# The first tiles of an S4 + int4-FFN block: dequantized weights scaled in 64-column operations, products split by pass, and a new written-out order on five engines

## The chip, the cores and the metric

The kernel runs on one core of one Trainium2 chip, as one launch. The metric is the time of one execution in device microseconds; the figure for the kernel before is the median of three such times. A profiled execution gives, besides, a trace of every instruction and DMA with start and duration.

Engine names are those of the profile: PE is the matrix engine (PEld its weight loads), DVE the vector engine, ACT the scalar engine, POOL the GpSimd engine, SP the engine that issues the DMAs. Instructions of one engine run in the order in which they stand.

## The reference: what is computed

`x` has 2048 rows of 1024 columns. With `xn = layernorm(x)` the result is

```python
x = x + s4(xn) + ffn(xn)
# ffn: the weights are int4, in groups of 64 with a scale and a zero each
w = (w - zero[:, :, None]) * scale[:, :, None]
g = jnp.einsum('bsh,ih->bsi', x, Wg)
u = jnp.einsum('bsh,ih->bsi', x, Wu)
h = jax.nn.silu(g) * u
return jnp.einsum('bsi,hi->bsh', h, Wd)
```

`s4` is a causal convolution of each row with a kernel of length 1024 made from S4 parameters, plus `D * xn`. The inner size of the FFN is 2752, that is 21 tiles of 128 rows of the weights (`j` = 0 to 20) and one half tile ("mix").

## The kernel before

**Precision.** Each fp32 operand is kept as a pair of fp16 numbers, high and low part. A product is three matmuls ("passes", `PASS = ((0, 0), (0, 1), (1, 0))`): weight high times x high, weight high times x low, weight low times x high. A pair is made by a cast on ACT (high) and a subtraction on DVE (low = value minus high).

**Stages.** (1) Rows of x are loaded, normalized and turned so that the hidden dimension lies on the partitions. (2) Gate and up products for all `j`: `j` = 0 and 1 as plain matmuls, from `j` = 2 on by a Strassen-like scheme with seven products over 2x2 blocks. (3) The convolution. (4) The down product. From stage 2's middle to the end, an order of the engines is written out or made by a planner; the change does not touch it.

**The first tiles.** The change is in the first 46 us. Here the first four x tiles (128 rows each, `n0` to `n3`, 512 KB) and the first four weight granules (`raw0` to `raw3`, 256 KB each; granules 0 and 1 are `j` = 0, granules 2 and 3 are `j` = 1, one per half of the contraction, `kq`) are made on the engines as follows.

- x tile `t`: `norm_stat(t)` on DVE (two bn_stats, one aggregate, and for `t` < 4 two small operations), a power on POOL, `scaled_x` on ACT, eight 128x128 transposes on PE into two PSUM banks, `early_hi(t)` (two casts on ACT), `early_lo(t)` (two subtractions on DVE).
- granule `gi`: `unpack` on DVE (two integer operations of 512 columns), scaling, eight transposes on PE, `early_w_hi` on ACT, `early_w_lo` on DVE.
- Scaling has three forms before: `scale_v` on DVE (two operations over all 1024 columns, with the scales broadcast, granules 0 and 3), `scale_part` on DVE (two operations over the first 12 groups, granule 1), and `scale_a` on ACT (one operation for each group of 64 columns, with scale and bias as one number per partition). `scale_a` and `scale_part` need `scale_c`, three small operations on POOL.
- `product(s, kq)`: the 24 matmuls of 128 columns of x tile `s` with granule `kq` of `j` = 0, for gate and up, with all three passes of each weight tile together. `j` = 1 follows as one block, `gate_up_plain(1, 0, 0, ...)`, 48 matmuls of 512 columns.

x tiles 4 to 15 go another way: `norm_stat` (DVE), power (POOL), `norm_hi` (ACT), `norm_lo` (DVE), and two DMA transposes for each tile on SP's queue.

**What sets the order.** Between `V.pin = A.pin = SP.pin = PE.pin = True` and `... = False` every operation of those engines is issued behind the one before it in the source: the order is the one written in the program (lines 941 to 1039 of before). POOL is not pinned. Behind this block a scheduler places the instructions at build time up to about 195 us; from there on a written order follows. Buffers limit it as well: `raw` and `w` have two buffers each, so the load of the third granule waits for the unpacking of the first, and the unpacking of the third for the transposes of the first; x tiles have eight buffers.

**Behind the block** come the rest of `j` = 0, 1 for x tiles 4 to 7 (`by_tile`), the mix granule, x tiles 8 to 15, `load_w` of granules 4 to 7 with DMA transposes (`wf<-nat` in the trace), and then `j` = 2 (`whole(2, 0)`), whose matmuls need granules 4 and 5, and `j` = 3, which needs 6 and 7.

Most operations are recorded through the class `Engine`, so that they all have line 82 (pinned) or 77 (not pinned) in the profile: the tile names tell them apart. `xt` and `wt` are the PSUM banks of the transposes, `wf` the turned weights, `x` the turned x, `n` the loaded x, `g` and `u` the gate and up banks, `nat` the weight pairs ahead of the DMA transposes.

Of the kernel before, what the change touches and what calls it, by code (L numbers as in the profile page):

```python
# [26 lines left out]
I32 = mybir.dt.int32  # L27
# [60 lines left out]
def build(nc, tc, x, xp, raw_d, sz_d, par_d, vct_d, tab_d, csrow_d, out):  # L88
# [3 lines left out]
    with es:  # L92
# [20 lines left out]
        def bank(name, tag="ps"):  # L113
            return psp.tile([P, 512], F32, tag=tag, name=name, **({} if tag == "ps" else {"bufs": 2}))

        V, A = Engine(tc, nc.vector), Engine(tc, nc.scalar)
        SP, G, PE = Engine(tc, nc.sync), nc.gpsimd, Engine(tc, nc.tensor)
# [32 lines left out]
        def xtile(cp, f):  # L150
            if (cp, f) not in xf:
                home, tag = (uxp, "ux") if f in (0, 1, 3) else (utp, "ut")
                xf[cp, f] = home.tile([P, 2, 4, 512], F16, tag=tag, name=f"x{cp}_{f}")
            return xf[cp, f]
# [17 lines left out]
        def fetch(*ts):  # L172
            for t in ts:
                xin[t] = utp.tile([P, 2048], F32, tag="ut", name=f"n{t}")
                for i in range(2 if t == 0 else 1):
                    part = slice(512 * i, 512 * i + 512) if t == 0 else slice(0, 1024)
                    SP.dma_start(xin[t][:, part], xp[t * P : (t + 1) * P, part])
# [38 lines left out]
        def turned(src, name):  # L216

            ps = bank(name).rearrange("p (a b) -> p a b", b=P)
            for b in range(4):
                PE.transpose(ps[:, b], src[:, P * b : P * b + P], ident)  # L220
            return ps

        def pair_hi(src, hi, name):
            ps = turned(src, name)
            A.copy(hi, ps)
            return ps
# [10 lines left out]
        def early_hi(t):  # L237
            xv, _ = halves(t)
            for i in range(2):
                f, sl = (3, 1, 7, 0)[2 * (t // 4 % 2) + i], slice(t % 4 * P, t % 4 * P + P)  # L240
                d = xtile(t // 8, f)
                early_x[t, i] = d[:, :, :, sl], pair_hi(xv[:, i], d[:, 0, :, sl], f"xt{t}_{i}")

        def early_lo(t):
            for i in range(2):
                d, ps = early_x.pop((t, i))
                los[t] = V.tensor_tensor(d[:, 1], ps, d[:, 0], ALU.subtract)
# [52 lines left out]
        with ea:  # L300
# [3 lines left out]
            def load_raw(gi):  # L304
                raw = wtemp("raw", [P, 16, 32], I32, f"raw{gi}")
                ld = SP
                ld.dma_start(raw, raw_d[gi].rearrange("p (a b) -> p a b", a=16))
                sz = wtemp("sz", [P, 2, 16], F32, f"sz{gi}")
                ld.dma_start(sz, sz_d[gi])
                return raw, sz  # L310
# [14 lines left out]
            def scale_v(w, sz):  # L325

                w3 = w.rearrange("p a b -> p (a b)")[:, 0:1024].rearrange("p (a b) -> p a b", a=16)
                bc = lambda k: sz[:, k].unsqueeze(2).to_broadcast([P, 16, 64])
                V.tensor_tensor(w3, w3.bitcast(I32), bc(1), ALU.subtract)
                V.scalar_tensor_tensor(w3, w3, WS, bc(0), ALU.mult, ALU.mult)  # L330

            def scale_c(gi, sz):

                G.tensor_scalar(sz[:, 0], sz[:, 0], WS, None, ALU.mult)  # L334
                G.tensor_tensor(sz[:, 1], sz[:, 1], sz[:, 0], ALU.mult)
                G.tensor_scalar(sz[:, 1], sz[:, 1], -1.0, None, ALU.mult)
                return sz

            def scale_part(w, sc, n):

                w3 = w.rearrange("p a b -> p (a b)")[:, 0 : 64 * n].rearrange("p (a b) -> p a b", a=n)
                bc = lambda k: sc[:, k, 0:n].unsqueeze(2).to_broadcast([P, n, 64])
                V.tensor_tensor(w3, w3.bitcast(I32), bc(0), ALU.mult)
                V.tensor_tensor(w3, w3, bc(1), ALU.add)
# [23 lines left out]
            def early_w_hi(gi, w):  # L368

                for i in range(2):  # L370
                    a = slice(4 * i, 4 * i + 4) if gi != G_MIX else slice(16 + 4 * i, 20 + 4 * i)
                    hi = wtile(0 if gi == G_MIX else gi)[:, a]
                    src = w.rearrange("p a b -> p (a b)")[:, 512 * i : 512 * i + 512]
                    early_w[gi, i] = pair_hi(src, hi, f"wt{gi}_{i}"), hi

            def early_w_lo(gi):
                for i in range(2):
                    ps, hi = early_w.pop((gi, i))
                    a = slice(8 + 4 * i, 12 + 4 * i) if gi != G_MIX else slice(16 + 4 * i, 20 + 4 * i)
                    V.tensor_tensor(wtile(1 if gi == G_MIX else gi)[:, a], ps, hi, ALU.subtract)  # L380
# [3 lines left out]
            def wtile(gi):  # L384
                if gi not in wft:
                    wft[gi] = wfp.tile([P, 28, P], F16, tag="wf", name=f"wf{gi}")
                return wft[gi]
# [196 lines left out]
            def plain(ps, w, cp, c, ts=slice(0, 512), kq=None, ends=None):  # L584


                xt = [xtile(cp, f) for f in ((3, 1), (7, 0))[c]]
                ks = [k for k in range(8) if kq in (None, k % 4 // 2)]
                first, last = ends or (0 in ks, 7 in ks)
                for k in ks:  # L590
                    for n, (wi, xi) in enumerate(PASS):
                        PE.matmul(ps[:, ts], w(k, wi), xt[k // 4][:, xi, k % 4, ts],
                                  start=(first and k == ks[0] and n == 0), stop=(last and k == ks[-1] and n == 2),
                                  **({"skip_group_check": True} if ends else {}))
# [104 lines left out]
            def plain_banks(j, cp, c):  # L699
                nm = f"{j}_{cp}{c}"  # L700
                return bank("g" + nm, "B"), bank("u" + nm, "D")

            def plain_part(banks, cp, c, wf, ts=slice(0, 512), kq=None, ends=None):
                for m, ps in enumerate(banks):
                    plain(ps, lambda k, wi: wf[k % 4 // 2][:, 8 * wi + 4 * m + k // 4 * 2 + k % 2, :], cp, c, ts, kq, ends)
# [238 lines left out]
            V.pin = A.pin = SP.pin = PE.pin = True  # L944
            busy, ones = bank("busy"), ident.bitcast(F16)
            for _ in range(24):
                PE.matmul(busy[:, 0:256], ones[:, 0:128], ones, start=True, stop=True)
            wt = {j: [wtile(2 * j), wtile(2 * j + 1)] for j in range(2)}
            first = plain_banks(0, 0, 0)

            def product(s, kq):
                plain_part(first, 0, 0, wt[0], slice(s * P, s * P + P), kq, ((s, kq) == (0, 0), (s, kq) == (3, 1)))

            fetch(0)
            rawt[0] = load_raw(0)
            rawt[1] = load_raw(1)
            fetch(1, 2)
            rawt[2] = load_raw(2)
            fetch(3)
            rawt[3] = load_raw(3)  # L960
            fetch(4, 5, 6, 7)
            rawt[G_MIX] = load_raw(G_MIX)
            xtile(0, 7)
            norm_stat(0)
            w0, s0 = unpack(0)
            scaled_x(0, 2)
            scale_v(w0, s0)
            w1, s1 = unpack(1)
            c1 = scale_c(1, s1)
            early_hi(0)  # L970
            early_w_hi(0, w0)
            norm_stat(1)
            scale_a(w1, c1, range(12, 16))
            early_lo(0)
            early_w_lo(0)
            product(0, 0)
            scaled_x(1)
            scale_part(w1, c1, 12)
            early_hi(1)
            fetch(8)  # L980
            early_w_hi(1, w1)
            early_lo(1)
            norm_stat(2)
            w2, s2 = unpack(2)
            c2 = scale_c(2, s2)
            product(1, 0)
            early_w_lo(1)
            product(0, 1)
            product(1, 1)
            scale_a(w2, c2, range(5))  # L990
            scaled_x(2)
            scale_a(w2, c2, range(5, 7))
            early_hi(2)
            fetch(9)
            w3, s3 = unpack(3)
            norm_stat(3)
            early_lo(2)
            product(2, 0)
            scale_a(w2, c2, range(7, 8))
            scaled_x(3)  # L1000
            scale_v(w3, s3)
            scale_a(w2, c2, range(8, 10))
            early_hi(3)
            fetch(10)
            product(2, 1)
            early_lo(3)
            scale_a(w2, c2, range(10, 16))
            early_w_hi(3, w3)
            product(3, 0)
            product(3, 1)  # L1010
            norm_stat(4)
            early_w_hi(2, w2)
            norm_stat(5)
            early_w_lo(3)
            early_w_lo(2)
            norm_hi(4)
            norm_hi(5)
            norm_lo(4)
            norm_stat(6)
            norm_hi(6)  # L1020
            norm_lo(5)
            fetch(11)
            norm_stat(7)
            norm_hi(7)
            norm_lo(6)
# [5 lines left out]
            early_w_hi(G_MIX, wq)  # L1031
# [5 lines left out]
            V.pin = A.pin = SP.pin = PE.pin = False  # L1037
# [19 lines left out]
            h0a = plain_h(first, 0, 0, 0)  # L1057
            h1a = gate_up_plain(1, 0, 0, wt[1])
# [557 lines left out]
```

## Time and profile before

| | us |
|---|---|
| median of three executions | 1281.69 (1280.97 to 1282.39) |
| the profiled execution, its own time | 1286.51 |
| its span in the trace | 1284.7 |
| PE busy | 1259.7 (98%) |
| DVE busy | 1020.2 (79%) |
| ACT busy | 676.5 (53%) |
| POOL busy | 184.3 (14%) |
| end of the first 46 us block on PE (last `u` matmul of `j` = 1, x tiles 0 to 3; start of the next block) | 45.89 |

PE is busy for nearly the whole span, so the time is PE's work plus PE's waits: 25 us of the span are not busy. A busy PE is not a PE at its peak: the clock it was granted is a column of its own. An engine's idle time is of interest only where PE, or a chain that PE later waits for, hangs on it.

### The profile page before, as it was taken

What the parts mean: (1) busy time and instruction counts of PE and PEld (TensorE: products, weight loads), DVE (VectorE), ACT (ScalarE), POOL (GpSimd) and SP (SyncE); (2) the same over time, 40 slices, a digit from 0 to 9 for tenths busy, and PEclk for the clock granted to TensorE, in tenths of its full rate; (3) what the DMA queues carried; (4) which work ended last, traced back from release to release, by engine and by line L of the source; (5) the groups of instructions that cost most, each with busy time, mean ns of one, the idle gap of its engine ahead of it and who ended that gap; (6) DMA issues with size and microseconds to landing.
All of it is one profiled execution on the core that took longest, in us unless ns stands there. A gap on an engine that the chain in (4) does not pass through costs nothing. (4 is left out here: it accounts for less than half of the span.)

```text
span 1284.7 us, 21385 instructions
## 1 busy us (share of the span) xinstructions
PE 1259.7 (98%) x8098; PEld 760.0 (59%) x8098; DVE 1020.2 (79%) x1391; ACT 676.5 (53%) x1219; POOL 184.3 (14%) x280
## 2 busy tenths in 40 slices
PE   7999899999999999999998999999999999999998
PEld 6644344444444444444443444467678888888887
DVE  7789975788888788779787886657669889779792
ACT  6777665665757656676576575620205433343330
POOL 2330010000010000101010001100000130366440
PEclk8999999999999999999998999999999999999999
DMA  6792829788895969799998998866868777999981
GB/s 233 195 209 50 184 92 207 191 227 207 207 252 133 266 148 247 192 224 248 238 243 198 260 246 185 251 231 200 307 201 317 254 236 217 257 288 257 289 175 50
DMA packets 358842, 276.59 MB, mean 215 GB/s; under 512 B 211851, under 2 KB 304851, under 8 KB 354643
## 3 DMA queue, kind: packets, MB, share of 16 engines
q1 hardware_dynamic: 336147, 263.17, 74.4%
q0 software_dynamic: 22016, 11.02, 7.1%
q8 instruction: 63, 1.03, 0.3%
q10 hardware_dynamic: 576, 1.05, 0.2%
q14 instruction: 40, 0.33, 0.1%
HBM read 132.88 MB, written 94.84 MB: 177 GB/s over the span
## 5 line engine op out<-in xcount | busy, mean ns | idle before, releaser
L82 PEld LDWEIGHTS <-wf 128*128 128x128 f16 x3000 | 287.3, 99 | 348.9 <-issue 11.5
L77 PEld LDWEIGHTS <-g 128*128 128x128 f16 x2940 | 287.6, 98 | 34.0 <-DVE g L77 0.6
L82 ACT ACTIVATE w<-w,sz 128x64 f32<-128x64 int32 x564 | 197.8, 428 | 66.8 <-DVE w L82 50.1
L82 PE MATMUL D<-x,wf 128*128 128x512 f16 x816 | 191.3, 385 | 2.2 <-ACT D L82 2.2
L77 PE MATMUL A<-b,g 128*128 128x256 f16 x1680 | 186.0, 273 | 0.3 <-DVE g L77 0.3
L82 PE MATMUL A<-x,wf 128*128 128x512 f16 x792 | 177.9, 380 | 5.0 <-DMA wf<-nat 4.6
L82 PE MATMUL C<-x,wf 128*128 128x512 f16 x804 | 179.1, 379 | 0.0
L77 ACT CAST g<-a 128x2560 f16<-128x2560 f32 x42 | 97.4, 2325 | 135.8 <-PE A L77 50.4
L82 DVE TENSOR_TENSOR w<-w 128x256 f32<-128x256 f32 (+1 forms) x244 | 132.7, 545 | 39.4 <-ACT w L82 32.3
L77 PEld LDWEIGHTS <-wf 128*128 128x128 f16 x960 | 86.0, 98 | 95.6 <-DMA wf<-nat 5.7
L77 DVE TENSOR_TENSOR g<-a,g 128x2560 f16<-128x2560 f32 x42 | 118.2, 2820 | 27.5 <-ACT g L77 27.5
L1468 POOL DMA_DIRECT2D out<-o x64 | 77.9, 2019 | 308.1 <-DVE o L77 288.3
L334 POOL TENSOR_SCALAR sz<-sz 128x16 f32<-128x16 f32 x43 | 19.4, 450 | 627.8 <-DMA sz<-in_sz 551.7
L82 ACT CAST nd<-w 128x896 f16<-128x896 f32 x70 | 65.3, 933 | 83.5 <-DVE w L82 70.0
L77 PE MATMUL D<-b,g 128*128 128x256 f16 x840 | 94.1, 273 | 0.0
L82 PE MATMUL B<-x,wf 128*128 128x512 f16 x396 | 90.9, 379 | 0.1
L82 DVE TENSOR_TENSOR nd<-w,nd 128x896 f16<-128x896 f32 x70 | 76.0, 1086 | 9.1 <-ACT nd L82 9.1
L82 ACT CAST nat<-w 128x896 f16<-128x896 f32 x62 | 55.3, 936 | 33.4 <-ACT B L82 17.0
L77 PEld LDWEIGHTS <-x 128*128 128x128 f16 x672 | 54.3, 98 | 20.9 <-issue 2.4
L82 DVE TENSOR_TENSOR nat<-w,nat 128x896 f16<-128x896 f32 x62 | 64.8, 1084 | 1.1 <-ACT nat L82 1.1
L77 DVE SCALAR_TENSOR_TENSOR p<-cv,p 128x512 f32<-128x512 f32 x32 | 22.0, 689 | 34.9 <-PE cv L77 23.4
L77 PE MATMUL cv<-band,x 128*128 128x256 f16 (+3 forms) x384 | 47.0, 272 | 2.0 <-DVE p L77 2.0
(181 smaller groups left out, 1451.1 us busy)
## 6 DMA issues: line engine op xcount, KB each, us to landing
a<-HF SPq DMA_DIRECT2D x28, 1280.0 KB, 7.4
WD<-nd SPq DMA_DIRECT2D x70, 448.0 KB, 4.0
b<-WD SPq DMA_DIRECT2D x49, 640.0 KB, 6.1
w<-SZT SPq DMA_DIRECT2D x80, 256.0 KB, 5.3
raw<-in_raw SPq DMA_DIRECT2D x65, 256.0 KB, 4.0
HF<-ha SPq DMA_DIRECT2D x54, 256.0 KB, 3.2
HF<-s SPq DMA_DIRECT2D x40, 256.0 KB, 3.2
HF<-hb SPq DMA_DIRECT2D x36, 256.0 KB, 3.2
```

What stands on the lines that cost most here:

```text
L77: return method(*args, **kw)
L82: self.last = method(*args, **kw)
L334: G.tensor_scalar(sz[:, 0], sz[:, 0], WS, None, ALU.mult)
L1468: G.dma_start(dst, o[:, q], accum_op=ALU.add)
```

## The change

It changes how the first four granules are scaled, in which order the first tiles are worked on, and how their products are cut; the mathematics stays.

- **Scaling.** `scale_v` and `scale_part` are gone. `scale_g` on DVE does one operation for each group of 64 columns: `w * a + b`, with `a` and `b` as one number per partition each. The groups are shared out anew: granule 0 has 16 groups on DVE; granule 1 has 8 on DVE and 8 on ACT; granule 3 has 10 and 6; granule 2 has 15 and 1. `scale_c` (POOL) is now needed for granules 0 and 3 too.
- **Loads.** The scales of granule 0 (`sz0`) go between the two halves of x tile 0, `raw0` behind both; x tile 1 is loaded ahead of `raw1`; granule 3 and x tile 3 are loaded ahead of granule 2.
- **Products** take a list of passes, so that the passes with a low part can stand behind others. `j` = 1 (`wide`) is cut into four pieces by granule and pass, inside the pinned block.
- **Order.** The order of all of these is new. x tile 3 and granule 3 come ahead of x tile 2 and granule 2. POOL is pinned as a fifth engine. The transposes of x tile 0 use banks of the tags B and D. 20 more filler matmuls (`busy`): 32 at the start, 12 ahead of the first product. `h0a` moves into the block.

By instruction: DVE loses 6 scaling operations (two of 1024 columns twice, two of 768) and gains 49 of 64 columns; ACT loses 5 of 64 columns; POOL gains 6 small ones; PE gains 20 filler matmuls with their weight loads; SP has the same 757 rows in another order. Behind about 195 us the order is the same on every engine.

```diff
-        SP, G, PE = Engine(tc, nc.sync), nc.gpsimd, Engine(tc, nc.tensor)
+        SP, G, PE = Engine(tc, nc.sync), Engine(tc, nc.gpsimd), Engine(tc, nc.tensor)
...
-            def scale_v(w, sz):
-
-                w3 = w.rearrange("p a b -> p (a b)")[:, 0:1024].rearrange("p (a b) -> p a b", a=16)
-                bc = lambda k: sz[:, k].unsqueeze(2).to_broadcast([P, 16, 64])
-                V.tensor_tensor(w3, w3.bitcast(I32), bc(1), ALU.subtract)
-                V.scalar_tensor_tensor(w3, w3, WS, bc(0), ALU.mult, ALU.mult)
...
+            def scale_g(w, sc, groups):
+
+                wv = w.rearrange("p a b -> p (a b)")
+                for g in groups:
+                    V.tensor_scalar(
+                        wv[:, 64 * g : 64 * g + 64], wv[:, 64 * g : 64 * g + 64].bitcast(I32),
+                        sc[:, 0, g : g + 1], sc[:, 1, g : g + 1], ALU.mult, ALU.add,
+                    )
...
-            for _ in range(24):
-                PE.matmul(busy[:, 0:256], ones[:, 0:128], ones, start=True, stop=True)
+            turning(32)
...
+            half_x = lambda i: SP.dma_start(xin[0][:, 512 * i : 512 * i + 512], xp[0:P, 512 * i : 512 * i + 512])
             fetch(0)
-            rawt[0] = load_raw(0)
+            half_x(0)
+            rawt[0] = load_raw(0, lambda: half_x(1))
+            fetch(1)
             rawt[1] = load_raw(1)
-            fetch(1, 2)
+            fetch(2)
+            rawt[3] = load_raw(3)
+            fetch(3)
             rawt[2] = load_raw(2)
-            fetch(3)
-            rawt[3] = load_raw(3)
             fetch(4, 5, 6, 7)
             rawt[G_MIX] = load_raw(G_MIX)
...
+            c0 = scale_c(0, sz[0])
             norm_stat(0)
-            w0, s0 = unpack(0)
             scaled_x(0, 2)
-            scale_v(w0, s0)
-            w1, s1 = unpack(1)
-            c1 = scale_c(1, s1)
+            w0 = unpack(0)[0]
+            scale_g(w0, c0, range(8, 16))
+            c1 = scale_c(1, sz[1])
+            scale_g(w0, c0, range(0, 8))
+            turn_w(0, w0)
+            norm_stat(1)
+            w1 = unpack(1)[0]
+            early_w_hi(0)
+            turn_x(0)
+            turning(12)
+            first = plain_banks(0, 0, 0)
+            early_w_lo(0)
             early_hi(0)
...
+            scale_a(w1, c1, range(8, 16))
+            scale_g(w1, c1, range(0, 8))
             early_lo(0)
+            w3 = unpack(3)[0]
+            product(0, 0, 2)
+            turn_w(1, w1)
+            c3 = scale_c(3, sz[3])
+            product(0, 0, 0, 1)
+            norm_stat(3)
             scaled_x(1)
...
+            product(1, 0, 1)
+            turn_x(3)
+            fetch(9)
+            scale_g(w3, c3, range(0, 8))
+            scale_a(w3, c3, range(10, 16))
+            early_hi(3)
             scaled_x(2)
+            product(1, 1, 0, 1)
+            early_lo(3)
+            norm_stat(4)
+            turn_w(3, w3)
+            early_w_hi(3)
+            norm_stat(5)
+            product(3, 1)
+            w2 = unpack(2)[0]
+            turn_x(2)
+            fetch(10)
+            product(3, 0)
             early_hi(2)
             early_lo(2)
+            norm_stat(6)
+            second = plain_banks(1, 0, 0)
+            wide(1, 0, 1)
+            scale_g(w2, c2, range(8, 16))
+            scale_g(w2, c2, range(0, 7))
+            norm_hi(4)
+            scale_a(w2, c2, range(7, 8))
             product(2, 0)
+            norm_hi(5)
+            early_w_lo(3)
             product(2, 1)
+            turn_w(2, w2)
             norm_lo(4)
             norm_hi(6)
             norm_lo(5)
+            early_w_hi(2)
+            norm_lo(6)
+            wide(1, 2)
+            early_w_lo(2)
+            wide(0, 0, 1)
+            h0a = plain_h(first, 0, 0, 0)
+            wide(0, 2)
             fetch(11)
             norm_stat(7)
             norm_hi(7)
...
-            h0a = plain_h(first, 0, 0, 0)
-            h1a = gate_up_plain(1, 0, 0, wt[1])
+            h1a = plain_h(second, 1, 0, 0)
```

In the program as built, DVE's order of the block after `product(1, 0, 0)` follows the same list; ACT has `h1a`'s Silu (which reads the last piece of `wide`) ahead of `norm_hi(7)`; SP has the store of `h1a` ahead of the two DMA transposes of x tile 7.

## The prediction

> **What bounds the kernel now.** I read the busy time by stages first. The stages are the first two, the written-out first block (to 46 us), what follows it, the four waits behind 131 us, and the long stretch to 477.
>
> ```profile
> 0.00:10.00 10.00, 6.97 (x40) 4.85 (x40) 5.77 (x12) 4.94 (x9) 4.52 (x13) 1.00 0.79 250
> 10.00:20.00 10.00, 7.01 (x56) 6.62 (x57) 8.10 (x15) 5.77 (x12) 1.26 (x4) 0.66 0.78 283
> 20.00:36.00 16.00, 13.61 (x191) 12.28 (x189) 14.69 (x31) 13.14 (x30) 4.01 (x11) 1.00 0.40 137
> 36.00:46.00 10.00, 10.00 (x50) 4.58 (x49) 6.52 (x11) 7.85 (x8) 2.81 (x6) 1.00 0.62 128
> 46.00:131.00 85.00, 85.00 (x542) 44.76 (x540) 75.61 (x109) 63.38 (x117) 15.71 (x36) 1.00 0.74 162
> 131.00:155.00 24.00, 20.76 (x94) 8.62 (x93) 23.56 (x30) 12.61 (x23) 0.00 (x0) 1.00 0.90 206
> 155.00:477.00 322.00, 321.59 (x1533) 147.53 (x1531) 257.17 (x417) 203.45 (x443) 21.75 (x58) 1.00 0.77 190
> ```
>
> The columns are PE, PEld, DVE, ACT, POOL, then PE's granted clock. PE lacks 8.4 us in the first 36 and none to 131; there it lacks 3.2 while DVE is full (23.56 of 24). From 155 to 477 PE is full again, so what is won or lost by 155 stays. The timeline of PE shows who is late at 131:
>
> ```profile
> 131.75 0.82 PE L77 MATMUL A<-x,wf 128*128 128x512 f16 x3 [0.24 <-DMA wf<-nat]
> 133.84 0.82 PE L77 MATMUL A<-x,wf 128*128 128x512 f16 x3 [1.26 <-DMA wf<-nat]
> 151.35 0.82 PE L77 MATMUL A<-x,wf 128*128 128x512 f16 x3 [0.86 <-DMA wf<-nat]
> 153.57 0.82 PE L77 MATMUL A<-x,wf 128*128 128x512 f16 x3 [0.75 <-DMA wf<-nat]
> ```
>
> PE waits here for the turned weights of granules 4 to 7. PE's own gain is therefore lost at this place unless the chain that makes them moves too. By the timelines of DVE and ACT that chain goes back without a break: DVE has hardly a gap from 83.94 (`norm_lo(15)`) to 148; before it `norm_stat`, POOL, `norm_hi` and `norm_lo` wait for one another in a loop; the loop begins with `norm_hi(8)` (54.25), behind the mix granule's 16 scalings on ACT (from 47.43), behind `norm_hi(7)` (45.21). So the question is when ACT starts `norm_hi(7)`.
>
> **The change part by part.** DVE's timeline prices the block:
>
> ```profile
> 5.34 0.21 DVE L82 TENSOR_SCALAR rs<-mv 128x1 f32<-128x1 f32 x2
> 5.47 0.75 DVE L82 TENSOR_SCALAR w<-raw 128x512 int32<-128x512 int32 x2
> ...
> 9.85 1.29 DVE L82 BATCH_NORM_STATS2 st<-n 128x6 f32<-128x512 f32 x2 [0.41 <-DMA n<-in_xp]
> ...
> 11.55 1.28 DVE L82 TENSOR_TENSOR x<-xt,x 128x512 f16<-128x512 f32 x2
> 12.74 1.28 DVE L82 TENSOR_TENSOR wf<-wt,wf 128x512 f16<-128x512 f32 x2
> ...
> 268.35 0.35 DVE L82 TENSOR_SCALAR s4n<-s4n,s4p 128x256 f32<-128x256 f32 x1
> 268.62 0.76 DVE L82 TENSOR_SCALAR w<-raw 128x512 int32<-128x512 int32 x2
> ```
>
> The first number is the start, the second the time from start to last end; operations overlap, so I price by starts. `norm_stat` takes 1.70 (9.85 to 11.55; 1.44 for tiles from 4 on, 30.86 to 32.30), a low pair 1.19, an `unpack` 0.67 (22.53 to 23.20).
>
> *The 64-column operation, T.* No row has it. Two operations of one column take 0.13, so 0.065 each; one of 512 columns 0.335; a column costs 0.53 ns. The only wide operation with a per-partition number (268.35) holds the next one off for 0.27; less 192 columns that is 0.17, so its number costs 0.07. The new form has two numbers. Bounds: 0.10 if they load beside the operation ahead; 0.24 if the second costs as much as the first; 0.32 if nothing overlaps (0.35 - 0.10 + 0.07). I take 0.17, the row it is nearest to.
>
> On the other side stands the Trainium skill, VectorE: DVE Perf Modes, section The TRN2 errata: a fixed cost per instruction, hence few large operations. Its 58 cycles plus half a cycle per column make 0.094 us for 64 columns, its measured 150 cycles 0.19; T by these would give a gain of 5.2 or 1.9 us below.
>
> *DVE.* Six operations go: two `scale_v` of 2.40 and `scale_part` of 2.01, together 6.8. 49 T = 8.3 come. DVE gets 1.5 us more work, and what changes the end is the order. In the built order DVE is never held from its first `unpack` on: each cast that it needs ends 0.7 us or more ahead (ACT has its pairs of casts at 0.5 each half; the closest are the casts of granule 1, ending 17.1, needed 17.8). From there to the first low half of x tile 2, which PE needs: four unpacks 2.7, three full `norm_stat` 5.1, two short 2.9, five low pairs 5.95, half a pair 0.6, and 34 of the 49 scalings (16 + 8 + 2 + 8): 17.25 + 34 T = 23.05.
>
> *The start.* `sz0` comes ahead of x tile 0's second half, whose issue moves by one (0.47 on SP). Landing is by bandwidth (0.98 between the halves before), so the delay lies between 0 and 0.47; I take 0.13, the size of a 16 KB load beside 256 KB in 0.98, doubled. The first `unpack` starts at 5.6. POOL's `scale_c(0)` stands ahead of the power of tile 0: 0.9 (12.10 to 13.00) when DVE is not on SBUF, 3.1 when it is (6.42 to 9.49). From `sz0`'s landing at about 4.5 (issue 1.20 plus the median 3.3) it ends between 5.4 and 7.6, with DVE's first scaling at 6.3 behind it; at 4.5 DVE does bn_stats, beside which the short price holds (24.28). I take nothing, and at worst 1.3.
>
> *x tile 1 sooner.* It removes the 0.41 at 9.85; one 256 KB load less in front is worth 0.8 at the 310 GB/s of that stretch, so it lands near 9.0, and `norm_stat(1)` is due at 5.6 + 0.7 + 16 T = 9.0. Nothing is left over.
>
> *PE.* From 28.65 it runs through: `wide(1, 0, 1)` 16 x 0.216 = 3.46, two products 48 x 0.056 = 2.69, eight transposes 0.92, `wide(1, 2)` 1.73, `wide(0, 0, 1)` 3.46, `wide(0, 2)` 1.73: 13.99, end 42.65 (durations: 22 matmuls 36.39 to 41.14, 12 in 0.67 at 32.17). Covers: granule 2's last scaling on DVE is at 33.3, due 34.8; its low pair at 39, due 40.9. Before, the same point is 45.89: 3.2 us sooner. The 32 and 12 fillers lie in time in which PE waits for DVE: without that cover 20 more would cost 3.9 (0.195 each, 24 in 4.68).
>
> *Clock.* In 10 to 20 us PE was granted 0.66, after gaps of 1.92 and 0.93; 22 matmuls and 16 transposes cost about 2.4 us more there. In the new order DVE sets PE's pace to 28.65, so I count nothing. The Trainium skill (TensorE: Matmul & The Clock Gate, Part 1) has half clock after an idle window of 3.4 us, which the fillers would avoid; by it, too, no term changes.
>
> *New waits.* ACT: `h1a`'s Silu, which needs `wide(0, 2)`, stands ahead of `norm_hi(7)`; ACT idles from 37 to 42.65 with it, and `norm_hi(7)` starts at 43.3 (0.6 for the Silu) instead of 45.21: 1.9 gained of PE's 3.2. SP: the store of `h1a` (44) stands ahead of x tile 7's transposes, which need `norm_lo(7)` (46.7) anyway. `raw2` waits for the second unpack (11.5) with x tiles 4 to 7 behind; four loads at 1.87 issue and 6.3 landing are there by 20, due 25. The mix granule's load waits for the third unpack (16); it is due at 42.
>
> *To 155.* The loop to `norm_lo(15)` has the same operations, and shifts by 1.9. Behind it, DVE's built order has one half-tile operation of the mix (0.7) less ahead of granule 7's low pairs: 2.6. PE is there 3.2 + 3.1 of waits early, so the chain decides.
>
> *Sum.* Gain = 8.4 - 34 T, with T = 0.17: 2.6 us. The span goes from 1284.7 to 1282.1, the profiled execution from 1286.51 to 1283.9. That execution is 4.8 above the median of the runs; the difference is put on the median: 1281.69 - 2.6 = 1279.1, or 0.20%. A measurement of this kernel tells about 0.2% (2.6 us) from no change.
>
> **The rivals.**
>
> A. *The per-partition numbers load beside the operation ahead*: T = 0.10, gain 5.0, 1276.7. For it: the two 1-column operations start 0.07 apart though each lasts 0.15. Against: the 0.27 at 268.35. `norm_stat(1)` would then wait for x tile 1, up to 0.9.
>
> B. *Both numbers are paid one after the other*: T = 0.24, gain 0.2, 1281.5, no change. For it: ACT's 64-column scalings, with two numbers, take 0.34 each, while the column part is 0.05.
>
> C. *Slower: DVE is the bound of the block, and 49 small operations cost more than six large ones save.* Place: the chain from the first `unpack` to x tile 2's low half. It decides from T = 0.247 on; at 0.32 the block's end lies at 47.7, `norm_hi(7)` starts 3.2 us late, and 0.7 come back: 2.5 slower, 1284.2. For it: DVE is busy 14.69 of 16 us before. Against: rows overlap by 0.08 everywhere.
>
> D. *The block ends sooner and nothing comes of it*: the four waits at 131 grow by what PE gains, as the chain of granules 4 to 7 does not move: 1281.7. For it: those waits. Against: `norm_hi(7)` had nothing else ahead of it.
>
> **How the numbers follow.** My forecast (T near 0.17) 40 in 100; A 18, B 22, C 16, D 4. Waits further on (8 us in all behind 155, at six places) may shift by 1.5 either way. Faster by over 0.2%: 22 of the 40, A's 18, 2 of B: 0.42. Slower by over 0.2%: 13 of C, 4 of B, 1 of the 40: 0.18. Within: 0.40. The range goes from A with half a wait more (1275.5) to C (1284.5); the forecast's own is 1277.5 to 1281.
>
> **What would show it.** T is read at once from the 16 operations of granule 0. Right: `wide` from about 28.7, the next block's last piece at 42.7, `norm_hi(7)` near 43.3 behind an idle ACT, `norm_lo(15)` near 82, waits at 131 to 155 of 3.1 to 4. Wrong: DVE waits inside the block, or a T beyond 0.24, or waits behind 155 that were not there.

## The result: 1287.8 us, slower by 0.45%

The median of four executions is 1287.80 us (1286.13 to 1288.49) against 1281.68 for the kernel before on the same chip: a ratio of 1.0045, 95% interval 1.0033 to 1.0057. The forecast was 1279.1, with a range up to 1284.5.

The two profiled executions don't show this in their spans (1284.7 before, 1284.4 after). That of after was the fastest of its four. That of before was 4.8 us above its median: a second profile of the same kernel (1282.75, span 1281.0) is ahead of it by 0.7 to 1.1 up to 658 us and by 3.8 from 820 us on, mostly because the wait near 800 is 0.5 shorter and has no low clock behind it. So I compare rows up to 477 us. Two landmarks serve for all kernels: the first `mix` matmul (67.89 and 67.21 in the two profiles of before), which closes the work on x tiles 0 to 7, and the first `s4s` matmul (305.83 and 305.01), which lies behind all the early waits. After the change they start at 72.15 and 310.81: 4.3 and 5.0 later than in the profile that the prediction shows.

The stages of the profile after, columns as in the prediction:

```profile
0.00:10.00 10.00, 6.27 (x32) 4.28 (x32) 4.64 (x17) 3.30 (x5) 3.01 (x16) 1.00 0.78 242
10.00:20.00 10.00, 9.35 (x69) 7.46 (x70) 9.90 (x31) 7.36 (x17) 1.73 (x5) 0.83 0.65 209
20.00:36.00 16.00, 14.93 (x176) 11.80 (x174) 15.79 (x47) 14.18 (x24) 5.09 (x14) 1.00 0.52 187
36.00:46.00 10.00, 10.00 (x88) 6.42 (x86) 9.72 (x19) 3.94 (x6) 0.57 (x2) 1.00 0.65 86
46.00:131.00 85.00, 82.51 (x513) 44.12 (x511) 69.02 (x98) 61.46 (x109) 18.42 (x41) 0.98 0.70 157
131.00:155.00 24.00, 22.12 (x101) 9.35 (x98) 24.00 (x33) 14.55 (x28) 0.00 (x0) 1.00 0.85 178
155.00:477.00 322.00, 319.50 (x1512) 146.12 (x1513) 257.01 (x415) 203.30 (x440) 23.52 (x58) 1.00 0.78 192
```

DVE is now full from 10 to 46, as forecast. What is new stands in the fifth row: PE lacks 2.5 of 85 us between 46 and 131, where it lacked nothing, and its clock is 0.98. PE's timeline shows where:

```profile
32.00 1.67 PE L82 MATMUL g<-x,wf 128*128 128x512 f16 x7 [0.51 <-DVE x L82]
...
53.98 0.61 PE L77 MATMUL u<-x,wf 128*128 128x128 f16 x8
56.91 0.27 PE L77 MATMUL g<-x,wf 128*128 128x128 f16 x2 [2.32 <-DMA x<-n]
...
57.70 0.49 PE L77 MATMUL g<-x,wf 128*128 128x128 f16 x6 [0.18 <-DMA x<-n]
...
58.18 1.49 PE L77 MATMUL u<-x,wf 128*128 128x128 f16 x12
59.46 1.49 PE L77 MATMUL g<-x,wf 128*128 128x128 f16 x12
...
61.79 5.34 PE L77 MATMUL g<-x,wf 128*128 128x512 f16 x24
```

The rows at 56.91 to 59.46 are the products of x tile 7 with `j` = 0, the last in the part of the next block that goes by x tiles. PE waits 2.50 for the DMA transposes of that tile, and then twelve matmuls take 1.28 (58.18 to 59.46) where they took 0.67. Before, the same products began without a wait:

```profile
54.85 0.83 PE L77 MATMUL g<-x,wf 128*128 128x128 f16 x12
...
57.53 5.34 PE L77 MATMUL g<-x,wf 128*128 128x512 f16 x24
```

The block itself ended level: its last matmuls end at 46.32, with twelve of the next block (0.67) already in between, so 45.65 against 45.89. The part by x tiles took 11.64 before (45.89 to 57.53). When tile 7's products are due (54.43: eight matmuls at 0.056 from 53.98) 8.78 of it is done; the remaining 2.86 take until 61.79, that is 7.36: 2.5 of waits and 2.0 of slow matmuls on top. -0.24 + 4.5 = 4.26, the whole of the first landmark. The remaining 0.7 are the four waits for `wf<-nat`, 3.87 instead of 3.11.

SP's queue tells why tile 7 was late. After the change:

```profile
48.40 0.52 SPq L82 DMA_DIRECT2D n<-in_xp  x1
49.01 0.88 SPq L77 DMA_DIRECT2D HF<-h  x2
49.94 0.46 SPq L77 DMA_DIRECT2D raw<-in_raw  x1
50.50 5.13 SPq L82 DMA_TRANSPOSE x<-n  x2
```

and before:

```profile
46.59 3.11 SPq L82 DMA_TRANSPOSE x<-n  x2
49.79 0.53 SPq L77 DMA_DIRECT2D HF<-h  x1
50.37 2.66 SPq L82 DMA_TRANSPOSE x<-n  x2
```

Tile 7's transposes are issued only 0.13 later, but right behind x tile 11's load (512 KB), two stores and one load of 256 KB each. Their two issues take 5.13 instead of 2.66, and they land at 56.9 and 57.7. Before, one store stood there.

DVE's timeline holds the forecast quantity T, and the start:

```profile
5.88 0.69 DVE L82 BATCH_NORM_STATS2 st<-n 128x6 f32<-128x512 f32 x1 [1.69 <-DMA n<-in_xp]
...
6.98 0.75 DVE L82 TENSOR_SCALAR w<-raw 128x512 int32<-128x512 int32 x2
7.83 3.67 DVE L82 TENSOR_SCALAR w<-w,sz 128x64 f32<-128x64 int32 x16
11.43 1.27 DVE L82 BATCH_NORM_STATS2 st<-n 128x6 f32<-128x512 f32 x2
...
48.98 1.22 DVE L82 TENSOR_TENSOR n<-n 128x1024 f16<-128x1024 f32 x1 [1.70 <-ACT n L82]
...
90.38 1.22 DVE L82 TENSOR_TENSOR n<-n 128x1024 f16<-128x1024 f32 x1 [1.04 <-ACT n L82]
```

T is (11.43 - 7.83) / 16 = 0.225. The first `unpack` starts at 6.98, not 5.6. `norm_lo(7)` (48.98) and `norm_lo(15)` (90.38, before 83.94) are the last two rows. ACT's timeline shows how the late x tile 7 reaches the second of them:

```profile
58.43 0.58 ACT L82 CAST wf<-wt 128x512 f16<-128x512 f32 x1 [3.70 <-PE wt L82]
58.91 1.24 ACT L82 ACTIVATE n<-n,rs 128x1024 f32<-128x1024 f32 x1
```

The mix granule's last cast waits 3.70 for PE, where its transposes stand among the products of x tile 7. Behind that cast `norm_hi(8)`, the start of the loop, begins at 58.91 instead of 54.25.

### The profile page after: what moved, and what is told of

It is laid out like the page before. It is cut to its first block, busy times and chain, and to the rows that moved or that the text cites. A ratio compares the mean times of both kernels' runs of the same rounds, so it can differ in the third digit from the quotient of the medians.

```text
span 1284.4 us, 21472 instructions
## 1 busy us (share of the span) xinstructions
PE 1260.7 (98%) x8118; PEld 761.9 (59%) x8118; DVE 1023.9 (80%) x1434; ACT 675.4 (53%) x1214; POOL 185.9 (14%) x286
## 5 line engine op out<-in xcount | busy, mean ns | idle before, releaser
L82 PE MATMUL D<-x,wf 128*128 128x512 f16 x816 | 187.5, 380 | 0.9 <-ACT D L82 0.9
L77 POOL TENSOR_SCALAR sz<-sz 128x16 f32<-128x16 f32 x80 | 38.5, 483 | 618.7 <-DMA sz<-in_sz 544.3
```

Of the source, the lines that this page charges most:

```text
L77: return method(*args, **kw)
L82: self.last = method(*args, **kw)
```

## The experiments

Theory Q: the loss is x tile 7's transposes, late because of what is queued ahead of them. Theory D: DVE's longer chain makes everything late, tile 7 included. All ratios are to the kernel before, timed on the same chip beside each group; "mix" and "s4s" are the landmarks of the profiled execution.

| run | what differs | ratio, 95% interval | median; profiled execution, us | mix | s4s |
|---|---|---|---|---|---|
| before, second profile | nothing | - | -; 1282.75 | 67.21 | 305.01 |
| after | the change | 1.0045 [1.0033, 1.0057] | 1287.80; 1286.13 | 72.15 | 310.81 |
| x7_first | tile 7's transposes ahead of stores | 1.0016 [1.0006, 1.0025] | 1284.24; 1282.00 | 68.57 | 307.74 |
| sz0_behind | scales of granule 0 later | 1.0039 [1.0026, 1.0051] | 1286.77; 1288.02 | 72.87 | 311.37 |
| wide_scale | broadcast scaling | 1.0020 [1.0011, 1.0029] | 1284.11; 1284.17 | 71.64 | 308.46 |
| stat7_sooner | `norm_stat(7)` sooner; by it, tile 7's transposes ahead of stores too | 1.0025 [1.0014, 1.0035] | 1285.10; 1286.99 | 71.12 | 308.33 |
| all_four | these four together | 1.0019 [1.0009, 1.0030] | 1284.66; 1286.84 | 67.52 | 307.07 |
| wide_x7 | broadcast, tile 7 first | 1.0006 [0.9995, 1.0018] | 1283.07; 1286.55 | 67.60 | 308.37 |
| wide_x7_f11 | and x tile 11 behind it | 1.0029 [1.0013, 1.0045] | 1285.31; 1285.19 | 65.94 | 306.93 |
| mended | and scales of granule 0 later | 1.0022 [1.0013, 1.0030] | 1284.12; 1284.59 | 65.88 | 306.78 |
| mend_mix | and the mix granule's operations later | 0.9997 [0.9988, 1.0006] | 1281.31; 1282.17 | 65.50 | 305.60 |
| before_g | before, 64-column scaling alone | 1.0027 [1.0015, 1.0038] | 1285.89; 1284.79 | 70.65 | 309.57 |
| before_mix | before, mix operations later | 0.9999 [0.9989, 1.0008] | 1282.25; 1282.25 | 67.62 | 305.81 |

The landmarks and rows are of the one profiled execution, whose own time lies up to 3.5 us from the median of its kernel (wide_x7). So the ratios say which kernel is faster; a difference of a us or two between the landmarks of two kernels is shown for these executions alone.

**The kernel before once more.** 

> The kernel before, once more, for its profile: the one shown was 4.8 us above the median of its runs. If that lay in its waits behind 680 us (2.89, 1.25 and 2.22, each with a lower clock behind it), a second profile has smaller ones there and a span near 1280, while everything up to 477 us is as it was: block end 45.9, x tile 7's products without a wait, four waits of together about 3.1 us between 131 and 155.

Measured: 1282.75, span 1281.0. Between 131 and 153 the waits are 2.84, and behind 680 they are 2.66, 1.23 and 1.72, hardly smaller. Most of the difference is the clock: between 800 and 810 it was 0.83 in the first profile and full in this one, between 10 and 20 it was 0.66 and 0.83.

**x tile 7 first.** 

> The changed kernel with x tile 7's two DMA transposes ahead of the stores of h00 and h1a and ahead of granule 5's load on SP's queue; PE, DVE, ACT and POOL have the same order. Theory Q (the transposes land late because 1 MB of stores and loads was queued just ahead of them: 50.50 to 57.7): they land near 54.5, PE's wait of 2.32 + 0.18 at 56.9 goes, and with it the half clock behind it (about 2.0), ACT starts norm_hi(8) near 55.5 instead of 58.91, and the time falls by 3.5 to 4.5 us, to about 1283.5. Theory D (the DVE chain alone makes them late: norm_lo(7) ends at 50.20, and a transpose can't start before): the issue moves by less than 0.3, the wait stays above 2, and the time stays within 1 us of 1287.8.

```diff
 def emit(cp, j, f, src):
-    SP.dma_start(HF[cp][f, :, j // 2, :], src)
+    with tc.issue_after(turn7[7].ins) if (cp, j) in ((0, 0), (0, 1)) else nullcontext():
+        SP.dma_start(HF[cp][f, :, j // 2, :], src)
```

(`turn7[7]` is tile 7's second transpose; granule 5's load has the same condition.) Measured: 1284.24 against 1281.81. PE's timeline:

```profile
54.83 0.27 PE L77 MATMUL g<-x,wf 128*128 128x128 f16 x2 [0.82 <-DMA x<-n]
...
55.75 0.50 PE L77 MATMUL g<-x,wf 128*128 128x128 f16 x6 [0.31 <-DMA x<-n]
...
56.20 0.83 PE L77 MATMUL u<-x,wf 128*128 128x128 f16 x12
56.87 0.83 PE L77 MATMUL g<-x,wf 128*128 128x128 f16 x12
```

Issued at 49.64, 0.86 sooner, the transposes land at 54.78 and 55.70, about 2 sooner. The wait falls from 2.50 to 1.13, and behind it twelve matmuls take 0.67 again. By the sum above the stretch costs 1.5 instead of 4.5, which is 3.0 of the 3.6 at the landmark; 0.6 is a start that came sooner in this execution. Q is right in its larger part. The 1.13 that stay fit D, since `norm_lo(7)` ends at 49.62 and the transposes are issued at once; x tile 11's load (512 KB), still queued just ahead of them, is a rival here, and a run below moves it.

**Scales of granule 0 behind the second half of x tile 0.** 

> The changed kernel with the scales of granule 0 loaded behind the second half of x tile 0 instead of between the halves; nothing else moves on any engine. If those scales are what held the half up (5.88 instead of about 4.4 for its bn_stats), DVE's first unpack starts at 5.6 to 5.8 instead of 6.98 and all DVE work of the block comes 1.2 to 1.4 us sooner, unless the scales now come too late: then the first scaling waits for POOL behind 7.2. Theory Q: x tile 7's transposes move with the rest, the wait stays at about 2.5, and the time falls by 1 to 1.5 us. Theory D: norm_lo(7) 1.4 sooner, the wait shrinks by the same 1.4 as PE does not go faster than DVE, time down by 1.4 to 3.

```diff
-SP.dma_start(sz, sz_d[gi])
 between()
+SP.dma_start(sz, sz_d[gi])
```

```profile
4.27 0.69 DVE L82 BATCH_NORM_STATS2 st<-n 128x6 f32<-128x512 f32 x1
...
5.98 0.76 DVE L82 TENSOR_SCALAR w<-raw 128x512 int32<-128x512 int32 x2 [0.52 <-DMA raw<-in_raw]
6.84 3.72 DVE L82 TENSOR_SCALAR w<-w,sz 128x64 f32<-128x64 int32 x16
```

The half tile lands 1.6 sooner, as before the change, so the 16 KB load had held it up. But the first `unpack` then waits for its weights: 1.0 us sooner, not 1.4. The time is 1286.77 where the whole change is at 1287.80, with intervals that overlap. In this execution PE's wait for x tile 7 grew to 3.09 and took the gain back (mix at 72.87), which neither theory had. In the seven profiles with the loads of the change the half tile's bn_stats start at 4.98 to 5.89 and `unpack` at 6.1 to 7.6; in the four with the scales behind, at 4.17 to 4.27 and 5.8 to 6.1. So the small load ahead of the half tile costs the first `unpack` 0.9 on average; against the four profiles with the old loads (5.5 to 5.7) the new ones lose 1.3.

**Broadcast scaling.** 

> The changed kernel with the scaling on DVE undone alone: each list of groups by two operations with broadcast numbers (as the kernel before did for granule 1), same order, same shares of DVE and ACT. By the rows of before (1.0 for 768 columns, 1.20 for 1024) the 49 operations of 0.225 (11.0 us) become 12 that take about 7.4; on the way to x tile 2's low half 7.65 becomes about 5.1. Theory D (DVE bounds the block, the price of the small operation decides): the low half of x tile 2 comes 2 to 2.5 us sooner, PE's block ends near 44, and the time falls by 3 or more. Theory Q: the block ends 2 to 2.5 sooner too, but the wait at x tile 7's products stays above 1.5, and the time falls by 1 to 2.5.

```diff
-for g in groups:
-    V.tensor_scalar(wv[:, 64*g : 64*g+64], ..., sc[:, 0, g:g+1], sc[:, 1, g:g+1], ALU.mult, ALU.add)
+V.tensor_tensor(w3, w3.bitcast(I32), bc(0), ALU.mult)
+V.tensor_tensor(w3, w3, bc(1), ALU.add)
```

```profile
8.09 2.82 DVE L82 TENSOR_TENSOR w<-w,sz 128x512 f32<-128x512 int32 x4
...
33.18 2.64 DVE L82 TENSOR_TENSOR w<-w,sz 128x512 f32<-128x512 int32 x4
```

Granule 0 takes 2.74 instead of 3.60, granule 2's 15 groups 2.55 instead of 3.31: 0.17 for a group instead of 0.225. From the first `unpack` to `norm_lo(7)` that is 1.7 us in all, and 1.0 to x tile 2's low half, since DVE now waits in between: less than expected. In this execution `unpack` waited for its load until 7.23, so `norm_lo(7)` came 1.5 sooner. The wait at x tile 7 stayed (2.72, with the slow matmuls behind it), as Q has it. Yet the time fell by 3.7 to 1284.11, more than Q allowed. At the first landmark 0.5 of it shows and at the second 2.4: two of the waits between 131 and 158 are gone (2.59 left of 3.87), with `norm_lo(15)` at 87.84 instead of 90.38. So the scaling acts there too, on the chain that makes granules 4 to 7.

**`norm_stat(7)` ahead of `norm_lo(4)`.** 

> The changed kernel with norm_stat(7) ahead of norm_lo(4) on DVE and norm_hi(7) ahead of h00's Silu on ACT; the mix granule's unpack and norm_lo(6) move behind granule 2's low half, and in the built order the two stores and granule 5's load now stand behind x tile 7's transposes. Theory Q+D (x tile 7 was late for two reasons: norm_lo(7) at 48.98, and 1 MB queued ahead of its transposes): norm_hi(7) starts near 40 instead of 46.62, the turns are issued at about 48.3 behind the six others and land by 53, no wait at x tile 7's products, norm_hi(8) near 54.5, and the time falls below that of the run with the transposes ahead of the stores alone (1284.2), to about 1282. Theory P (the place behind it binds: the weights of granules 4 to 7 come from a chain of DVE and ACT work that this does not shorten): the waits between 131 and 158 grow to 5 or more, and the time stays within 1 us of 1284.2.

Measured 1285.10, not below the 1284.24 with the transposes ahead of the stores alone: not as Q+D has it. `norm_hi(7)` started at 42.18, `norm_lo(7)` at 45.64, but the six transposes of x tiles 4 to 6 kept SP until 49.1, and x tile 11's load (512 KB) went out just ahead of tile 7's transposes. The first landed 5.95 after its issue, at 55.73; PE waited 1.81, and the half clock followed (0.57 from 57 to 61 us). `norm_hi(8)` came at 51.62, 2.6 ahead of before, without use: the waits between 131 and 158 are 2.7. P's time fits, its grown waits don't. At x tile 7 it is SP's queue that sets the time here, not DVE.

**The four together.** 

> All the mends together: scales of granule 0 behind the second half of x tile 0, scaling by broadcast operations, norm_stat(7) sooner, x tile 7's transposes ahead of the stores. If the losses found add up (start 0.4 to 1.0, scaling 1.7 to 2.4 on the way of DVE, x tile 7 3.6 or more), the block ends near 43.5, norm_lo(15) starts near 82 instead of 90.38, and the time is 1279 to 1280.5, below the kernel before (1281.8). If the chain that makes granules 4 to 7 binds, the block's gain turns up as waits of 5 us or more between 131 and 158, and the time is 1282 or more.

Measured 1284.66: they don't add up. (The profiled execution is the slowest of twelve.) `norm_hi(8)` starts at 49.38, over 4 us ahead of before, but `norm_lo(15)` at 82.72, only 0.5 to 1.2 ahead. In between, DVE waits for the load of x tile 15, which stands behind transposes on SP's queue:

```profile
75.24 1.29 DVE L82 BATCH_NORM_STATS2 st<-n 128x6 f32<-128x512 f32 x2 [2.66 <-DMA n<-in_xp]
```

and PE waits 3.5 between 131 and 136; the clock is 0.83 from 130 to 140, the drop coming behind these waits.

**The kernel before with 64-column scaling.** 

> The kernel before with one part of the change alone: its 44 groups on DVE (granule 0, 12 of granule 1, granule 3) by 64-column operations, old order and old loads. By the 0.225 found for one operation, granule 0 takes 3.6 instead of 2.40, granule 1's twelve 2.7 instead of 2.01, granule 3 3.6 instead of 2.40: 3.1 us more of DVE. Theory D (DVE sets the pace of the first tiles in the kernel before too): most of it shows, the block ends at 47.5 to 49 instead of 45.2 to 45.9, and the time rises by 2 or more. Rival: DVE is not full there (8.1 of 10 us between 10 and 20, 14.69 of the next 16) and hides it: up by less than 1.

```profile
7.39 3.69 DVE L82 TENSOR_SCALAR w<-w,sz 128x64 f32<-128x64 int32 x16 [1.16 <-POOL sz L338]
...
15.75 2.76 DVE L82 TENSOR_SCALAR w<-w,sz 128x64 f32<-128x64 int32 x12
```

Measured 1285.89 against 1281.90, 3.5 us by the ratio and 4 by the medians, and the block ends at 48.64: D is right for this kernel. Besides 3.61 and 2.7 instead of 2.40 and 2.01, DVE waits 1.16 for POOL's three small operations, which the old form doesn't need for this granule. The scaling form by itself, with POOL's wait, loses in the old order some 60% of what the whole change loses.

**Broadcast scaling and x tile 7 first.** 

> The changed kernel with two mends, broadcast scaling and x tile 7's transposes ahead of the stores. Each alone took about 3.6 us off the 1287.8. If they act at two places (scaling on DVE's chain up to 158 us, the queue on PE's wait at 56), they add up to 5.5 to 7, and the time is 1281 to 1282; if they act through the same wait, the second adds less than 1, and it stays above 1283.

Measured 1283.07: over broadcast scaling alone the second mend added 1.0 (1.8 by the ratios), between the two cases. PE's wait at x tile 7 is 0.88, but what was won by 131 (mix at 67.60) is partly lost in waits of 3.5 there, with half clock behind them (0.69 from 130 to 140). That profiled execution is the second slowest of its twelve.

**The price of the operation.** 

> A measurement of the 64-column operation, in the changed kernel: granule 0's 16 operations as they are (two per-partition numbers), granule 1's 8 with one number and one constant, granule 3's 10 with two constants, granule 2's in 128-column pieces with two numbers (14 groups, each piece with its first group's scale). So granules 1 to 3 are scaled wrongly: the time is not that of the computation, only the starts of the operations are read. By the prediction's working each number costs 0.07 and a column 0.53 ns: 0.225 becomes 0.155 with one number and 0.085 with none, and 128 columns with two take 0.26. If the small operation has a fixed price whatever its numbers are, the three forms of 64 columns lie within 0.02 of each other, and 128 columns with two numbers take 0.26 too.

```profile
8.49 3.66 DVE L82 TENSOR_SCALAR w<-w,sz 128x64 f32<-128x64 int32 x16
...
15.62 1.39 DVE L82 TENSOR_SCALAR w<-w,sz 128x64 f32<-128x64 int32 x8
...
24.75 0.90 DVE L82 TENSOR_SCALAR w<-w 128x64 f32<-128x64 int32 x8
...
32.95 1.86 DVE L82 TENSOR_SCALAR w<-w,sz 128x128 f32<-128x128 int32 x7
```

The last of each series lasts 0.31, 0.25, 0.19 and 0.33, so from start to start ((3.66 - 0.31) / 15 and so on): 0.223 with two per-partition numbers, 0.163 with one, 0.102 with none, and 0.255 for 128 columns with two. Each number costs 0.06 and they add; 64 more columns cost 0.03.

**x tile 11's load behind x tile 7's transposes too.** 

> The changed kernel with broadcast scaling, x tile 7's transposes ahead of the stores, and ahead of x tile 11's load (512 KB) as well; against the run with the first two mends only SP's queue differs. Theory Q (what is queued just ahead of the transposes makes them late): x tile 7's turns start about 0.6 sooner and land 1.5 to 2 sooner, the wait of 0.88 at its products goes, the time falls by about 1 from 1283.1. Theory D (norm_lo(7), ended at 48.31, sets it): the turns can't start before 48.4, the wait stays above 0.5, no change.

```diff
-fetch(11)
 norm_stat(7)
...
 norm_lo(7)
-fetch(12)
+fetch(11, 12)
```

At its place Q is right: issued at 47.45, the transposes land at 50.65 and 53.19, the wait is gone, and mix starts at 65.94, 1.7 sooner. Of that 0.9 is a block that ran sooner in this execution (`unpack` at 6.49 instead of 6.99, and on PE the first `wide` goes on at 29.98 instead of 30.86), and 0.8 is the queue: the second transpose lands 5.7 after the first issue instead of 6.5. But the time did not fall (1285.31, with executions from 1281.24 to 1288.30): the waits between 129 and 155 grew to 6.0. Against the run before it the difference is not settled; that nothing was won is.

**Four mends on SP and DVE.** 

> The same with granule 0's scales behind the second half of x tile 0: four mends, and PE, DVE, ACT and POOL in one order with the run before this one. By the run that moved these scales alone (1.0 less) another 0.4 to 1.0: 1281 to 1282, level with the kernel before. If the waits between 131 and 158 take it back (their sum was 3.5 with two mends, with 3 us of clock lost behind them), it stays at 1282.5 or more.

Measured 1284.12, the second case. x tiles 0 to 7 are done 1.3 to 2.0 us sooner than before, and it is given back, by PE's timeline,

```profile
129.43 0.82 PE L77 MATMUL A<-x,wf 128*128 128x512 f16 x3 [0.58 <-DMA wf<-nat]
131.63 0.82 PE L77 MATMUL A<-x,wf 128*128 128x512 f16 x3 [1.38 <-DMA wf<-nat]
133.67 1.46 PE L77 MATMUL A<-x,wf 128*128 128x512 f16 x3 [1.21 <-DMA wf<-nat]
...
152.31 0.82 PE L77 MATMUL A<-x,wf 128*128 128x512 f16 x3 [0.60 <-DMA wf<-nat]
...
154.53 0.82 PE L77 MATMUL A<-x,wf 128*128 128x512 f16 x3 [0.75 <-DMA wf<-nat]
```

because `norm_lo(15)` comes at 86.09, 2.2 to 2.9 later than before. ACT's and DVE's timelines:

```profile
84.37 0.61 ACT L77 CAST mpc<-msa 64x512 f16<-64x512 f32 x1 [3.20 <-DMA HF<-s]
```

```profile
85.02 0.69 DVE L77 TENSOR_TENSOR mpc<-msa,mpc 64x512 f16<-64x512 f32 x1 [3.92 <-ACT mpc L77]
86.09 1.23 DVE L82 TENSOR_TENSOR n<-n 128x1024 f16<-128x1024 f32 x1 [0.38 <-ACT n L82]
```

A cast of the mix granule waits for a buffer that a store on SP's queue frees, and x tile 15's casts stand behind it.

**The mix granule's operations behind `norm_lo(15)`.** 

> The run with four mends, and the mix granule's four operations for x tiles 0 to 7 on ACT and on DVE behind norm_hi(15) and norm_lo(15) instead of ahead of them. In the run with four mends ACT's cast of the mix (at 84.37, ahead of norm_hi(15)'s second half) waited 3.2 us for a buffer that the store of an s tile frees, and DVE's norm_lo(15) stood at 86.09, 2.9 later than in the kernel before, although the block had ended 1.3 us sooner. Theory E (the block's gain is lost there, on SP's queue): norm_lo(15) starts at 81 to 82, the waits between 129 and 155 fall from 4.5 to 2.5 or less, and the time falls by 1.5 to 3 from 1284.1, to about 1282. Theory F (the chain that makes granules 4 to 7 is limited by something behind 86 us, and the moved operations, 0.69 each, only lengthen it): the waits stay above 4 and the time stays within 1 us of 1284.1.

```diff
-for c in range(2):
-    mix_h(0, c, mix(0, c))
+mixes = [mix(0, c) for c in range(2)]
 norms(...)
+for c in range(2):
+    with tc.issue_after(A.last.ins), tc.issue_after(V.last.ins):
+        mix_h(0, c, mixes[c])
```

```profile
134.27 0.82 PE L77 MATMUL A<-x,wf 128*128 128x512 f16 x3 [0.19 <-DMA wf<-nat]
...
150.27 0.88 PE L77 MATMUL A<-x,wf 128*128 128x512 f16 x3 [2.88 <-DMA wf<-nat]
150.94 1.49 PE L77 MATMUL C<-x,wf 128*128 128x512 f16 x3
```

Theory E is right: `norm_lo(15)` starts at 80.68, the three waits at 129 to 134 are gone but for 0.19, and the time is 1281.31 against 1281.76, 2.8 below the run before it (3.2 by the ratios). It is level with the kernel before, no better: PE still waits 2.88 at 150 for granules 6 and 7, with 1.7 of half clock behind it, and the lead of 2.5 to 3.3 us over the two profiles of before that it had at 143 is spent. Why the weights of granules 6 and 7 come no sooner, though `norm_lo(15)` does, no run shows; DVE is full there (10.00 of 10 us between 140 and 150).

**The same move in the kernel before.** 

> The kernel before with the same four operations moved behind norm_hi(15) and norm_lo(15), nothing else. There the cast of the mix waited 0.4 only. Theory E: norm_lo(15) comes about 1.5 to 2.5 sooner (83.2 to about 81), and the time changes by no more than 1 us, since the operations moved are of about that length; if it falls by 2 or more, the place binds the kernel before too. Theory F: the waits between 131 and 153 grow by what is moved, 1 to 2.5 us slower.

Measured 1282.25 against 1281.76, ratio 0.9999 [0.9989, 1.0008]; `norm_lo(15)` at 81.53, the waits behind 131 3.7 instead of 2.84. No change, as E has it. None of the versions beats the kernel before.

## Why the prediction was wrong

**T was mis-sized.** The step took 0.17, "the row it is nearest to", a wide operation with one number, and left the second number without a price. It is 0.225, since each number costs 0.06: 0.102 + 2 x 0.061. That was rival B's reading (0.24). On the 34 operations of the chain the difference is 1.9 us.

**The start was mis-sized.** "0.13" for the small load between the halves of x tile 0 was 1.5 here: `unpack` at 6.98, before at 5.47. Over all profiles it is 1.3, of which 0.9 goes when the scales stand behind the half tile. That is beyond the step's own bound of 0.47, so its ground, "landing is by bandwidth", does not hold for this load; what delays it instead no run shows.

**The chain itself held.** 17.25 + 34 x 0.225 = 24.9, and the trace has 24.9 from 6.98 to the end of x tile 2's first low half (31.9, from where PE goes on at 32.00). PE's 13.99 from there took 13.75. DVE waited nowhere in it, as said; POOL's scales cost 0.2. With the two sizes put right the working gives a block that ends level, and so it did.

**SP's queue was costed by its issues alone.** The step said that `h1a`'s store stands ahead of x tile 7's transposes, "which need `norm_lo(7)` (46.7) anyway". The issue moved by 0.13 indeed, but the transfers queued with it moved the landing by over 2 us, and x tile 7 was the one x tile for which PE then waited. This wait and the half clock behind it are 4.5 of the 5.0 us at the second landmark, where the sum had put nothing; with the transposes ahead of the stores the time fell by 3.6. No rival had it. Rival C named the right side, but not through this: T stayed below its deciding point of 0.247. The three sizes, 1.9 for T, 1.4 for the start (6.98 instead of 5.6) and 4.5 here, make 7.8; between the forecast gain of 2.6 and the 5.0 lost at the second landmark lie 7.6. Undone, the three do not add up, as the runs above show.

**"The loop to `norm_lo(15)` shifts by 1.9" fell.** It doesn't shift as a whole: with `norm_hi(8)` over 4 us sooner it waits for x tile 15's load, and elsewhere for a buffer freed by a store, both on SP's queue. The run with four mends tests this step apart from the two sizes: its groups cost 0.17, its `unpack` starts at 6.06, its block ends at 42.97 and its `norm_hi(7)` starts at 43.42, close to the forecast's 42.65 and 43.3. Yet `norm_lo(15)` starts at 86.09 and not near 82, and the time is 2.5 above the kernel before and not 2.6 below. With `norm_lo(15)` at 80.68 it was level. So the forecast would have failed with T at its 0.17 as well, and rival D (4 in 100) describes what a mended version meets: the block 1.3 to 2.0 sooner, and that or more given back at 129 to 155. It was priced too low because its evidence against it, that nothing stood ahead of `norm_hi(7)`, says nothing of what stands behind.

**New waits on ACT.** That `h1a`'s Silu doesn't hold up `norm_hi(7)` was right: it ended at 45.97, and `norm_hi(7)` waited on until 46.62 for POOL, behind `norm_stat(7)` on the late DVE.

**A fixed price for each operation, and the clock.** The Trainium skill, VectorE: DVE Perf Modes, section The TRN2 errata, speaks against many small operations, and was right about the direction: 0.225 for a group against 0.17 in broadcast form. An estimate from its 58 cycles plus half a cycle per column (0.094 for 64 columns) meets the operation without per-partition numbers (0.102); an estimate from its measured 150 cycles (0.19) lies below the one with two (0.223). TensorE: Matmul & The Clock Gate, Part 1, has half clock after an idle window of about 3.4 us; here it came behind a wait of 2.32 and not behind 0.82 and 0.31. The prediction had a row of its own on this (0.66 of the clock behind gaps of 1.92 and 0.93), and weighed it for the block alone.

## What to carry to other kernels

When the order on one engine changes, follow the DMA queue as far as the first tile that has no reserve, and cost what is queued ahead of it by bytes, not by issues; a short wait there may cost nearly twice its length when the matrix engine's clock drops behind it (here 2.5 and 2.0). A small operation is priced by the form it really has: count its per-partition numbers. Before crediting a gain, look for the next place where every engine's work meets again: here any lead at 46 us had to pass a queue at 70 to 85 us and a full DVE to 150, and none did.

## What the runs showed of the hardware

- A 64-column DVE operation costs 0.102, 0.163 or 0.223 us from start to start with none, one or two per-partition numbers; 64 more columns add 0.03.
- A 16 KB load (128 bytes for each partition) between two 256 KB loads delayed what needs the second by 0.7 to 1.7 us from execution to execution.
- A pair of DMA transposes took 2.66 to issue behind one 256 KB store, and PE did not wait for it 4.5 us after its first issue; behind 1.28 MB of loads and stores it took 5.13 to issue and landed 6.4 and 7.2 us after. Behind one 512 KB load the first landed 4.0 to 6.0 and the second 6.1 to 7.0 after the first issue (four runs), behind other transposes alone 3.2 and 5.7 to 6.1 (three runs).
- Behind waits of PE the clock was halved after 2.32, 2.88 and after 1.38 + 1.21, not after 0.82 + 0.31. The length of the wait alone doesn't decide it: 1.20 at 137.87 after the change left the clock at 1.00, and so did 0.53 + 1.31 + 1.24 (129 to 134 us, the run that moves x tile 11's load), while 1.28 + 0.53 in the run with `norm_stat(7)` sooner was followed by 0.57 from 57 to 61.
